# An adaLN transformer block on one core: in seven of sixteen blocks, exponentials straight from query-by-key scores, turned on VectorE and gathered through DRAM

## The chip, the cores and the metric

The kernel runs on one core of a Trainium2 chip. A core has five engines that run side by side, each in its own order: TensorE (PE in the profile; its weight loads stand as PEld), VectorE (DVE), ScalarE (ACT), GpSimd (POOL) and SyncE (SP), which here issues nearly all transfers. Sixteen DMA engines move the data. An engine waits for another by semaphores. The metric is the time of one execution in microseconds (us); lower is better. Before the change the median of three runs is 3510.68 us (3505.79 to 3512.32).

## What is computed

A transformer block with adaptive layer norm, in float32: batch 8, sequences of 1024 rows, width 512, 16 heads of 32, hidden width 2048. The attention is causal.

```
mod = silu(condition) @ Wada + bada
sh_a, sc_a, gt_a, sh_m, sc_m, gt_m = split(mod, 6)
xm = layernorm(x, g1, be1) * (1 + sc_a) + sh_a
q, k, v = heads(xm @ Wqkv)
scores = where(causal, q @ k.T * hd ** -0.5, -inf)
x = x + gt_a * (softmax(scores) @ v @ Wproj + bproj)
xm = layernorm(x, g2, be2) * (1 + sc_m) + sh_m
x = x + gt_m * (gelu(xm @ W1 + b1) @ W2 + b2)
```

## The kernel before

The rows are cut into 16 blocks `n` of 512, two to each batch: the even block is a sequence's first half, the odd one its second. The queries of an even block see the keys of their own block (a triangle of ten 128x128 tiles per head), those of an odd block see 26 tiles. The 16 heads stand in four groups `g` of four heads; a group's four heads take the 128 partitions, 32 each.

*Linear work.* The projections and the MLP go by Strassen products over halves (`strassen`, `down`), each matmul group through the helper at line 217 into one of three PSUM banks. Weights come in pieces of 256 KB through a ring of eight (`fetch`, line 347, the tile `w`): a piece's load is issued when the piece eight places before it has been used. Pre-added pieces of weights lie in DRAM (`kept_...`). Normalized rows are turned for the products by 32x32 blocks on VectorE (line 700, tile `hat` to `xm`), stored to DRAM (`held`) and loaded back in another order.

*Attention before.* The scores are computed twice. First by query and key (`scores_at_once`, tile `sc`, matmuls at line 1595): VectorE adds the causal mask on the diagonal (line 1607) and takes the maximum of each row (line 1610). The maxima are split into three bf16 parts (`split_maxima`), transposed by matmuls into rows (`maxima_rows`, line 1648) and copied to `mrow`. Then the scores by key and query (`weights_T`, tile `st`): a bf16 matmul puts the negated maxima in (line 1674), an f32 one adds the scores (line 1686), one ScalarE activation takes the exponentials of up to 4 x 512 columns (line 1698) into a page `pT`, and GpSimd sets what lies behind the diagonal to zero (line 1703). `weigh` multiplies page and values into `po` (line 1726). GpSimd adds the pages up (line 1816), `finish` sums the result over keys by matmuls with ones (line 1747), copies sums and outputs out of PSUM, inverts the sums on VectorE in four pieces (line 1765) and multiplies on GpSimd (line 1790). The result takes the place of the queries, and `project_out` reads it.

`sc` and `st` share one buffer of four PSUM banks (`ps_st`, one buffer), `po` is one bank, and there are three pages (`free_p`) of 8 KB per partition. A unit of work is one part of 512 columns or two parts that add up to 512 (the triangle's rows of 384 and 128, or the 256s of two neighbouring groups): five units for two groups of an even block.

*What sets the order.* The order of every engine's instructions is written out by a planner in the kernel: estimated costs (`note`, `note_act`, `note_dma`) give each buffer a due time, and at each step the planner takes attention or linear work, whichever waits least, keeping to a rate between the two (`step_aside`, line 1457; `pace`, line 1899). On the chip each engine then works off its own list in order. All transfers stand in SP's list, so a transfer that has to wait holds back those behind it, weights among them.

```
    ps_st = ctx.enter_context(tc.tile_pool(name="ps_st", bufs=1, space=PSUM))
    RING = 8
    free_p = list(range(3))
    TRIANGLE = [[0], [1, 3], [2]]
```

Of the kernel before, what the change touches and what calls it, by code (L numbers as in the profile page):

```python
# [22 lines left out]
def kernel(  # L23
# [414 lines left out]
    cond_act = tmp.tile([P, TB], F32, tag="top", name="cond_act", bufs=1)[:B, :]  # L438
# [118 lines left out]

    def run_jobs(everything=False):
# [37 lines left out]
    def hurry():  # L596

        while jobs and due(jobs[0][1]) <= now["PE"] + 500:
# [882 lines left out]
    groups = [(n, g) for n in range(NB) for g in range(NC)]  # L1481
# [177 lines left out]
    free_p = list(range(3))  # L1659
    first_end, unadded = (0, NC - 1), []  # L1660
    outs, totals = {}, {}

    def weights_T(n, g, parts):
# [31 lines left out]
        slot = free_p.pop(0)  # L1695
# [40 lines left out]
    def finish(n, g):  # L1736
# [15 lines left out]
        free_p.extend([slot, *(held for *_, held in more)])  # L1752
        top = tmp.tile([P, TB], F32, tag="top", name=f"top_{n}_{g}", bufs=1)
        rec = tmp.tile([P, TB], F32, tag="rec", name=f"rec_{n}_{g}", bufs=1)
# [28 lines left out]

        def quotient():
            invert(3)
# [33 lines left out]
    def attend():  # L1819
        previous = None  # L1820
        for n in range(NB):
            h = blocks[n][1]
            slots = []
            mine = sum(exp_need(parts) for g in range(NC) for parts in weight_units(n, g))
            for g in range(NC):
                nxt = groups.index((n, g)) + 1
                n_slots = len(weight_units(n, g))

                over = n_slots - 1 if g % 2 == 0 else n_slots
                for k in range(n_slots):  # L1830
                    upto = len(units)
                    if nxt < len(groups):
# [4 lines left out]
                        if k == n_slots - 1 and nxt + 1 < len(groups):  # L1837
# [3 lines left out]
            stream["rate"] = planned_time(n) / mine * (0.7 if n == 0 else 1.0)  # L1841
# [32 lines left out]
    def close(n, g, parts, pT, slot, last):  # L1874

        until(lambda: n - blocks[n][1] + parts[-1][0] // NTT in valued)
        own, other = [[part for part in parts if (part[3] == g) == of] for of in (True, False)]
# [3 lines left out]
        elif parts[0][0] > 0 and (n, g) != first_end:  # L1881
            free_p.append(slot)
        if parts[0][0] == 0:
            totals[n, g] = (pT, slot)
            if (n, g) in shared:
# [3 lines left out]
                if (n, g) != first_end:  # L1889
                    free_p.append(slot)  # L1890
        if last:
            finish(n, g)

# [17 lines left out]
    needs = sum(exp_need(parts) for n in range(NB) for g in range(NC) for parts in weight_units(n, g))  # L1911
    needs += sum(score_need(*unit) for unit in units)
# [81 lines left out]
```

## Time and profile before

| | |
|---|---|
| median of three runs | 3510.68 us (3505.79 to 3512.32) |
| profiled execution | 3510.74 us |
| its span | 3509.0 us |
| mean granted TensorE clock | 0.998 |
| matmuls of scores by query and key, line 1595 | 329.5 us busy |
| matmuls of scores by key and query, line 1686 | 300.8 us busy |
| exponentials, line 1698 | 540.9 us busy on ScalarE |
| additions of pages, line 1816 | 1219.7 us busy on GpSimd |
| moved by the DMA engines | 491.10 MB, 140 GB/s over the span |

A group of the profile names the line, the engine, the operation, what is written and read, the shapes and the number of records; then the busy time, the mean time of one in ns, and the idle time of the engine just before it with what ended it. An f32 matmul stands as two records. A line of the timeline has start, duration, engine, line, operation and count, and in brackets the idle time before it. A line of the windows has the window, its length, busy time and records of PE, PEld, VectorE, ScalarE and GpSimd, and at its end the granted clock, the DMA engines' busy share and GB/s.

### The profile page before, as it was taken

To read this page: it belongs to the slowest core of one execution; us is meant where nothing else is said; L and a number is where in the kernel's file an instruction comes from. 1 tells how busy PE (TensorE), PEld (TensorE's weight loads), DVE (VectorE), ACT (ScalarE), POOL (GpSimd) and SP (SyncE) were. 2 spreads that over 40 slices of the span, in tenths; PEclk is the share of its full clock that TensorE was granted. 3 is DMA by queue.
4 is the path that set the end of the run, shared out by engine and by line. 5 is a ranking of instruction groups with operands and counts; after the bars stand their busy time and mean duration, and the time that the engine had idled before them with its cause. 6 is when DMAs were issued, how large, how long until landed. Compare 5 with 4: busy or idle time off the path is not lost.

```text
span 3509.0 us, 120365 instructions
## 1 busy us (share of the span) xinstructions
PE 3454.3 (98%) x54429; PEld 1724.0 (49%) x54429; DVE 2198.9 (63%) x2401; ACT 1212.4 (35%) x1276; POOL 2084.2 (59%) x2258
## 2 busy tenths in 40 slices
PE   8999999999999999999999999999999999999999
PEld 4444445445554545445454454544555444554445
DVE  5766676564666656665666566765666756656563
ACT  2335333342233423335223342333423343232531
POOL 3767846666366663756727576275753658537660
PEclk9999999999999999999999999999999999999999
DMA  6843444535545445363454534545354544443334
GB/s 212 263 137 104 137 115 140 142 107 159 142 125 156 119 147 153 119 170 115 137 157 130 155 117 144 150 137 148 116 155 137 165 122 146 128 136 101 96 121 140
DMA packets 328194, 491.10 MB, mean 140 GB/s; under 512 B 27260, under 2 KB 177596, under 8 KB 324100
## 3 DMA queue, kind: packets, MB, share of 16 engines
q1 hardware_dynamic: 327568, 483.39, 47.1%
q8 instruction: 428, 7.01, 0.8%
q14 instruction: 82, 0.67, 0.1%
q10 hardware_dynamic: 116, 0.03, 0.0%
HBM read 425.57 MB, written 55.64 MB: 137 GB/s over the span
## 4 chain that ended last, share of the span: by engine, by line
PE 83%; POOL 7%; DMA 3%; DVE 3%; ACT 1%; issue 1%; SPq 1%; ACTq 0%; DVEq 0%; POOLq 0%
PE bank L217 59%; PE sc L1595 8%; PE st L1686 6%; PE po L1726 6%; POOL pT L1816 4%; PE st L1674 2%; PE bank L1747 2%; DMA hat_m<-held_m 1%; DVE mx L1610 1%; POOL hT L170 1%; ACT pT L1698 1%; DMA held_m<-xm_m 1%; PE bank L1648 0%; POOL xr L170 0%; DMA w<-in_L_cond_Wqkv_dram 0%
## 5 line engine op out<-in xcount | busy, mean ns | idle before, releaser
L1816 POOL TENSOR_TENSOR pT<-pT,pT 128x256 f32<-128x256 f32 (+3 forms) x1254 | 1219.7, 1007 | 298.5 <-PE po L1726 181.6
L1698 ACT ACTIVATE pT<-st 128x2048 f32<-128x2048 f32 x288 | 540.9, 1878 | 1065.1 <-PE st L1686 959.8
L217 PE MATMUL bank<-w,hT 128*32 128x256 f32 x14336 | 823.7, 380 | 0.4 <-issue 0.4
L1610 DVE TENSOR_REDUCE mx<-sc 128x4 f32<-128x2048 f32 (+3 forms) x384 | 665.9, 1755 | 235.6 <-PE sc L1595 229.5
L217 PEld LDWEIGHTS bank<-w,hT 128*32 128x32 f32 x14336 | 446.7, 110 | 390.3 <-issue 105.8
L217 PE MATMUL bank<-xm_m,w 128*32 128x256 f32 x8192 | 498.6, 381 | 3.6 <-ACT xm_m L774 2.2
L217 PE MATMUL bank<-t_m,w 128*32 128x256 f32 x6144 | 382.4, 380 | 0.9 <-DVE t_m L786 0.6
L217 PEld LDWEIGHTS bank<-xm_m,w 128*32 128x32 f32 x8192 | 255.6, 110 | 231.2 <-issue 62.2
L1703 POOL TENSOR_SCALAR_AFFINE_SELECT pT<-pT 128x512 f32<-128x512 f32 x256 | 167.5, 672 | 331.9 <-ACT pT L1698 329.4
L1607 DVE TENSOR_TENSOR sc<-sc,mask 128x1024 f32<-128x1024 f32 (+1 forms) x160 | 162.8, 1018 | 293.3 <-PE sc L1595 237.8
L1595 PE MATMUL sc<-kT,qT 32*128 32x512 f32 (+3 forms) x3072 | 329.5, 521 | 4.3 <-ACT pT L1698 3.3
L1726 PE MATMUL po<-pT,v 128*32 128x512 f32 (+3 forms) x3048 | 301.6, 490 | 3.9 <-POOL pT L1703 3.9
L1686 PE MATMUL st<-qT,kT 32*128 32x512 f32 (+3 forms) x3072 | 300.8, 487 | 0.0
L217 PEld LDWEIGHTS bank<-t_m,w 128*32 128x32 f32 x6144 | 189.6, 110 | 172.9 <-issue 48.5
L1765 DVE RECIPROCAL rec<-rec 128x128 f32<-128x128 f32 x256 | 227.3, 922 | 48.2 <-ACT rec L1756 48.2
L217 PE MATMUL bank<-xm_a,w 128*32 128x256 f32 x3968 | 243.4, 382 | 0.4 <-DMA w<-in_L_cond_Wqkv_dram 0.4
L217 PE MATMUL bank<-w,qT 128*32 128x512 f32 x2048 | 237.0, 595 | 1.1 <-DMA w<-in_L_cond_Wproj_dram 0.7
L1595 PEld LDWEIGHTS sc<-kT,qT 32*128 32x128 f32 x3072 | 129.6, 183 | 188.2 <-issue 88.4
L208 DVE TENSOR_TENSOR hT<-bank,u_u 128x512 f32<-128x512 f32 x187 | 126.6, 686 | 105.8 <-PE bank L217 103.1
L217 PE MATMUL bank<-t_a,w 128*32 128x256 f32 x2944 | 183.2, 380 | 0.0
L217 PEld LDWEIGHTS bank<-xm_a,w 128*32 128x32 f32 x3968 | 123.5, 110 | 110.3 <-issue 29.3
L1115 ACT ACTIVATE hT<-hT,cols 128x512 f32<-128x512 f32 x256 | 164.7, 712 | 35.9 <-DVE hT L208 28.5
(243 smaller groups left out, 3404.0 us busy)
## 6 DMA issues: line engine op xcount, KB each, us to landing
w<-in_L_cond_W_dram SPq DMA_DIRECT2D x384, 256.0 KB
w<-kept_up_S SPq DMA_DIRECT2D x256, 256.0 KB
w<-kept_down_S SPq DMA_DIRECT2D x256, 256.0 KB
w<-kept_qkv_S SPq DMA_DIRECT2D x180, 256.0 KB
w<-in_L_cond_Wqkv_dram SPq DMA_DIRECT2D x147, 256.0 KB
hat_a<-in_x_dram SPq DMA_DIRECT2D x64, 256.0 KB
xr<-in_x_dram SPq DMA_DIRECT2D x32, 512.0 KB
w<-in_L_cond_Wproj_dram SPq DMA_DIRECT2D x64, 256.0 KB
```

The lines of the kernel that those rows point to most:

```text
L208: nc.vector.tensor_tensor(out, src, other, op)
L217: nc.tensor.matmul(ps[r, :], columns, rhs, start=start, stop=stop, skip_group_check=True)
L1115: nc.scalar.activation(hT[:, i, :], hT[:, i, :], AF.Gelu, bias=cols[:, O_B1 + f : O_B1 + f + 1])
L1595: nc.tensor.matmul(sc[:, j, c0 : c0 + w], qTs[n][r, gg, ts(qt, P)], keys_of(n, kh)[r, gg, :w], start=True, stop=True, skip_group_check=True,)
L1607: nc.vector.tensor_tensor(place, place, shape_of.to_broadcast(place.shape), ALU.add)
L1610: nc.vector.tensor_reduce(maxima[n, gg][:, kh, qt, :], sc[:, :, c0 : c0 + w], axis=AX.X, op=ALU.max)
L1686: nc.tensor.matmul(st[:, j, c0 : c0 + w], kT[r, gg, ts(k % NTT, P)], qT[r, gg, TB - w :], start=False, stop=True, skip_group_check=True,)
L1698: nc.scalar.activation(pT[:, :, :used], st[:, :, :used], AF.Exp, scale=scale)
L1703: nc.gpsimd.affine_select(diagonal, diagonal, pattern=[[0, HPG], [1, P]], compare_op=ALU.is_ge, fill=0.0, base=0, channel_multiplier=-1,)
L1726: nc.tensor.matmul(po[r, TB - w :], v[:, k % NTT, g * P + j * hd : g * P + (j + 1) * hd], pT[:, j, c0 : c0 + w], start=(k == 0), stop=last ...
L1765: nc.vector.reciprocal(some, some)
L1816: nc.gpsimd.tensor_tensor(into, into, pT[:, j, c0 : c0 + w], ALU.add)
```

## The change

Blocks 2, 4, 6, 8, 10, 12 and 14 (`by_rows`) take another way. Their scores are computed once, by query and key, with mask and maxima on VectorE as before. ScalarE takes the exponentials from there at once, one activation per head and part, with the row's negated maximum as bias, the running sum as a second output, and the columns written in an order that suits the turning. VectorE turns the page by 32x32 blocks in place, four transfers per part scatter it to an image in DRAM, and three pages per group are gathered from there with the keys on partitions. Their matmuls with the values follow (six visits per head and group where there were four). The sums stay with the rows: they are inverted as 128x16, turned, and go through DRAM into a tile of the output's layout, which multiplies the output once.

For these blocks the second scores, the maxima's rows, the zeroing and adding of pages on GpSimd, the column sums and the four inversions per group fall away. The odd block behind such a block takes its first page to the values only when the block's last group is finished. Of its pace, 0.6 of the block's linear work goes beside the row units and the rest beside the next block. `top` and `rec` become two halves of one tile, and small jobs of VectorE may run up to 2 us ahead of PE.

```diff
+    def by_rows(n):
+        return n > 1 and blocks[n][1] == 0
+
-    groups = [(n, g) for n in range(NB) for g in range(NC)]
+    groups = [(n, g) for n in range(NB) for g in range(NC) if not by_rows(n)]
...
     def run_jobs(everything=False):
+        run_row_jobs(everything)
         while jobs and (
-            everything or (now["DVE"] <= now["PE"] and due(jobs[0][1]) <= now["PE"])
+            everything or (now["DVE"] <= now["PE"] + 2000 and due(jobs[0][1]) <= max(now["PE"], now["DVE"]))
...
+            if by_rows(n):
+                attend_rows(n, previous)
+                previous = None
+                continue
...
     def close(n, g, parts, pT, slot, last):
         until(lambda: n - blocks[n][1] + parts[-1][0] // NTT in valued)
+        if blocks[n][1] and by_rows(n - 1):
+            until(lambda: (n - 1, NC - 1) in gathered)
...
+    def rows_unit(n, g, parts):
+        until(lambda: n in projected)
+        until(lambda: free_p and len(raws) < 2)
+        slot = take_slot()
+        raws.append(slot)
...
+        for qt, kh, c0, w, gg in parts:
+            for j in range(HPG):
+                r = slice(j * hd, (j + 1) * hd)
+                nc.tensor.matmul(
+                    sc[:, j, c0 : c0 + w], qTs[n][r, gg, ts(qt, P)], kTs[n][r, gg, :w],
+                    start=True, stop=True, skip_group_check=True,
+                )
...
+        nc.vector.tensor_tensor(place, place, shape_of.to_broadcast(place.shape), ALU.add)
...
+            nc.vector.tensor_reduce(mx[:, i, :], sc[:, :, c0 : c0 + w], axis=AX.X, op=ALU.max)
...
+        nc.vector.tensor_scalar(minus[:, :n_parts], mx[:, :n_parts], -scale, None, ALU.mult)
...
+            for j in range(HPG):
+                nc.scalar.activation(
+                    tile_of[:, j], sc[:, j, c0 : c0 + w].rearrange("p (k b x) -> p k b x", b=NTT, x=hd),
+                    AF.Exp, bias=minus[:, i, j : j + 1], scale=scale, accum_out=totals_of[n, gg][:, j, qt : qt + 1],
+                )
...
+        def turned():
+            nc.vector.transpose(raw, raw)
+            start(scatter())
...
+                for a in range(NTT):
+                    into = images[n, gg][qt // 2][:, qt % 2, a, :count, :]
+                    nc.sync.dma_start(
+                        into.rearrange("(b k) s e -> k b (s e)", k=hd),
+                        raw[ts(a, hd), at : at + HPG * w].rearrange("k (b f) -> k b f", b=NTT),
+                    )
...
+    def inverses(n, g):
...
+        nc.vector.reciprocal(some, some)
+        wide = some.rearrange("p j t -> p (j t)").unsqueeze(2).to_broadcast([P, HPG * NTT, hd])
+        nc.vector.transpose(both[:, 1, :].rearrange("p (y i) -> p y i", i=hd), wide)
...
+        nc.sync.dma_start(
+            rows.rearrange("j t a i -> a (j t) i"),
+            both[0:P:hd, 1, :].rearrange("a (y i) -> a y i", i=hd),
+        )
...
+            nc.sync.dma_start(both[ts(j, hd), 0, :], row.to_broadcast([hd, TB]))
...
+    def gather(n, g):
...
+        moves = (
+            [((both,), high[:, :, :, :2, :].rearrange("p t a s e -> p (t a) s e"), 2900)],
+            [
+                ((second,), high[:, 1, :, 2:, :], 1450),
+                ((first, 0), high[:, 0, :, 2, :], 730),
+                ((first, 1), low[:, 1, :, 1, :], 730),
+            ],
+            [((both, 0), low[:, :, :, 0, :].rearrange("p t a e -> p (t a) e"), 1450)],
+        )
...
+                yield [("image", n, g), SLOT, PAGE, *before], []
+                if free_p and not (pages and n not in issued):
+                    break
...
+            for at, source, ns in moves[i]:
+                nc.sync.dma_start(page[(slice(None), *at)], source)
...
+                    nc.tensor.matmul(
+                        state["out"][r, qt * P : qt * P + wide],
+                        vs[n][:, k, g * P + j * hd : g * P + (j + 1) * hd],
+                        page[:, rows_of, at, r],
...
+    def finish_rows(n, g, out):
+        key, into, by = ("att", n), qTs[n][:, g, :], inverse_rows.pop((n, g))
+        ready = due(["top", "po"])
+        if max(now["DVE"], ready) > max(now["ACT"], ready) + 2500:
+            nc.scalar.copy(into, out)
+            either(into, into, by, ALU.mult, ["top"], [key])
+        else:
+            nc.vector.tensor_tensor(into, out, by, ALU.mult)
```

More of the change, by code (lines that the diff above doesn't have):

```diff
@@ L1659, with count_slots, take_slot, give_slot @@
     free_p = list(range(3))
+    SLOT, PAGE = "a page", "a page to turned rows"
+    all_issued, pages = [True], []
+    def count_slots():
+        written[SLOT] = 0.0 if free_p else NEVER
+        written[PAGE] = NEVER if pages and not all_issued[0] else 0.0
+    def take_slot():
+        slot = free_p.pop(0)
+        count_slots()
+        return slot
+    def give_slot(slot):
+        free_p.append(slot)
+        count_slots()
     first_end, unadded = (0, NC - 1), []
@@ L1751, in finish @@
             note_pe(2 * COLUMN * w, "columns", [("acc", n, g), ("p", held)], [("l", bank)])
[L1752 to L1754 removed]
+        for one in (slot, *(held for *_, held in more)):
+            give_slot(one)
+        both = tmp.tile([P, 2, TB], F32, tag="top", name=f"top_rec_{n}_{g}", bufs=1)
+        top, rec = both[:, 0, :], both[:, 1, :]
         kr = "rec"
@@ L1782, in finish @@
             return
+        written["top used"] = NEVER
         def quotient():
+            written["top used"] = 0.0
             invert(3)
@@ new lines, in finish_rows @@
+    def finish_rows(n, g, out):
[3 more added lines that the diff above has]
+            nc.scalar.copy(into, out)
+            note_act(585, None, ["po"], [key])
+            either(into, into, by, ALU.mult, ["top"], [key])
+        else:
+            nc.vector.tensor_tensor(into, out, by, ALU.mult)
+            note("DVE", 690, ["po", "top"], [key])
+        written["spread", n, g] = 0.0
+        gathered.add((n, g))
+        if g == NC - 1:
+            written["attended", n] = 0.0
```

187 lines of the change are left out of this document (178 added, 9 removed).

## The prediction

> **What bounds the kernel now.** I read the engines' shares first, then PE's waits, then PE's groups by shape.
>
> ```profile
> span 3509.0 us, 120365 instructions
> PE 3454.3 (98%) x54429; PEld 1724.0 (49%) x54429; DVE 2198.9 (63%) x2401; ACT 1212.4 (35%) x1276; POOL 2084.2 (59%) x2258
> ```
>
> TensorE is busy for 3454.3 of 3509.0 us, and no other engine passes 63%. So a PE instruction that goes away takes its time off the end, and any wait given to PE instead is paid in full. The change is therefore a trade: matmuls taken from PE in seven blocks, against new waits of PE on a long way through the other engines and DRAM. The profiled execution took 3510.74 us (1.7 us around the span), the median of the runs is 3510.68: the sum below starts at 3510.7.
>
> **The change part by part. Matmuls that go.** The groups of PE by shape (busy us and mean ns of one):
>
> ```profile
> L1726 PE MATMUL po<-pT,v 128*32 128x512 f32 x1528 | 200.9, 597 | 3.2 <-POOL pT L1703 3.2
> L1686 PE MATMUL st<-qT,kT 32*128 32x512 f32 x1536 | 198.0, 590 | 0.0
> L1674 PE MATMUL st<-mrow,minus_ones 32*128 32x512 bf16 x768 | 76.0, 386 | 7.5 <-DVE mx L1610 6.9 <-ACT mrow L1654 0.4
> L1747 PE MATMUL bank<-pT,ones 128*32 128x512 f32 x512 | 75.0, 593 | 1.0 <-POOL pT L1816 0.9
> L1686 PE MATMUL st<-qT,kT 32*128 32x384 f32 x512 | 55.6, 509 | 0.0
> L1726 PE MATMUL po<-pT,v 128*32 128x384 f32 x504 | 52.8, 491 | 0.5 <-POOL pT L1703 0.5
> L1726 PE MATMUL po<-pT,v 128*32 128x256 f32 x512 | 39.7, 382 | 0.0
> L1686 PE MATMUL st<-qT,kT 32*128 32x256 f32 x512 | 33.1, 375 | 0.0
> L1648 PE MATMUL bank<-ident_b,mcols 128*32 128x128 bf16 x1024 | 26.2, 220 | 3.9 <-POOL mcols L1632 3.3 <-DVE hT L208 0.4
> L1726 PE MATMUL po<-pT,v 128*32 128x128 f32 x504 | 25.3, 273 | 0.2 <-POOL pT L1703 0.2
> L1686 PE MATMUL st<-qT,kT 32*128 32x128 f32 x512 | 24.9, 269 | 0.0
> L1674 PE MATMUL st<-mrow,minus_ones 32*128 32x384 bf16 x256 | 21.9, 332 | 1.0 <-DVE mx L1610 0.9
> L1674 PE MATMUL st<-mrow,minus_ones 32*128 32x128 bf16 x256 | 14.3, 214 | 0.0
> L1674 PE MATMUL st<-mrow,minus_ones 32*128 32x256 bf16 x256 | 12.7, 273 | 0.0
> ```
>
> Seven blocks of four groups lose, per group, four matmuls of each of the four widths; an f32 matmul stands as two records, so 224 records of each width go, and 112 of the bf16 ones. Busy per record is busy over count. Scores by keys (L1686): 224 x (0.129+0.109+0.065+0.049) = 78.6 us. Maxima into them (L1674): 112 x (0.099+0.086+0.050+0.056) = 32.5. Column sums (L1747): 224 x 0.146 = 32.8. Maxima turned to rows (L1648): 448 x 0.0256 = 11.5. The scores by queries stay, under another name. The weighted values are the same columns cut otherwise (896 records of 256 and 448 of 128 for 224 of each width): 69.4 + 22.5 against 81.5, +10.4. Together 145.0 us, as busy time. That is too much, since a group's tail overlaps the next group's head:
>
> ```profile
> 703.65 0.40 PE L1674 MATMUL st<-mrow,minus_ones 32*128 32x512 bf16 x4
> 703.87 1.03 PE L1686 MATMUL st<-qT,kT 32*128 32x512 f32 x8
> 704.83 0.64 PE L1726 MATMUL po<-pT,v 128*32 128x512 f32 x4
> ```
>
> Here a weight unit holds PE from 703.65 to 704.83, 1.18 us, where its busy times add up to 1.43: a factor 0.825, which makes 145 into 120. I take 120, and keep 145 as the upper end.
>
> **The way of a row unit.** Rows for its steps:
>
> ```profile
> L1610 DVE TENSOR_REDUCE mx<-sc 128x4 f32<-128x2048 f32 x192 | 439.8, 2291 | 232.3 <-PE sc L1595 229.5
> L1607 DVE TENSOR_TENSOR sc<-sc,mask 128x1024 f32<-128x1024 f32 x96 | 118.2, 1232 | 170.1 <-PE sc L1595 126.6 <-issue 21.6 <-ACT top L1759 13.4
> L1115 ACT ACTIVATE hT<-hT,cols 128x512 f32<-128x512 f32 x256 | 164.7, 712 | 35.9 <-DVE hT L208 28.5 <-POOL hT L170 6.7
> L677 ACT ACTIVATE rstd_m<-mv_m,eps 128x1 f32<-128x1 f32 x4 | 1.2, 295 | 17.9 <-DVE mv_m L675 12.2 <-DVE rstd_m L682 3.6 <-DVE offset_m L683 2.0
> ```
>
> The exponentials by query need a bias per head, so four or eight small ones replace one of 2048 columns. No row shows an exponential with a running sum; its bounds are 0.30 us (one column) and 0.71 (512 columns with a bias), in between by width, and I take 0.71, 0.61, 0.50, 0.40 for 512, 384, 256, 128. One unit then holds the only score buffer for its matmuls (1.1), mask (0.7 or 1.2), maxima (2.3 or 2.4) and exponentials (2.9 or 4.0): 7 us for one part, 9 for two, ten units 82 us a block. PE fills that with projections and MLP wherever the built order has some between.
>
> Behind it stand VectorE's turning of 2048 columns, the scatter to DRAM and the gathers. The nearest row is how the normalized rows go the same way, 1 MB out and back:
>
> ```profile
> 827.81 2.43 DVE L700 STREAM_TRANSPOSE xm_a<-hat_a 128x512 f32<-128x512 f32 x4
> 830.48 0.42 SPq L709 DMA_DIRECT2D held_a<-xm_a  x1
> 835.61 2.79 SPq L714 DMA_DIRECT2D hat_a<-held_a  x4
> 845.36 2.93 ACT L774 ACTIVATE xm_a<-hat_a,shifta,gaina 128x512 f32<-128x512 f32 x4 [2.62 <-DMA hat_a<-held_a]
> ```
>
> Turning four times 512 columns takes 2.43 us, and from the store's issue to data back 14.9. So from the end of a group's last score matmuls to its first page: 3.7 + 4.0 + 2.4 + 14.9 = 25 us (20 if SP is free, 35 if other transfers stand ahead).
>
> I weigh that against the built order of the changed kernel, taking each PE instruction start to start. In blocks 4 to 14 the work between a group's last score matmuls and its first page is 31 to 56 us: covered. In block 2 it is 13 us, because the output projection of block 1 stands there, itself behind block 1's last quotient; from the block's first row unit to the first page PE has 25 us of work where three units (9+7+9), turning and the round trip need 42. So PE stands 17 us there, and about 4 more at pages that come 3 us behind one another, since a second page is asked for only when the first has been used.
>
> **A standing PE costs more than its wait.** Granted clock is the third column from the end:
>
> ```profile
> 215.00:220.00 5.00, 2.33 (x16) 1.09 (x20) 3.90 (x3) 0.20 (x1) 4.68 (x8) 0.76 0.19 53
> 220.00:225.00 5.00, 5.00 (x26) 1.01 (x18) 3.05 (x3) 2.58 (x2) 5.00 (x4) 0.56 0.02 5
> 218.81 0.62 PE L1674 MATMUL st<-mrow,minus_ones 32*128 32x512 bf16 x4 [2.41 <-DVE mx L1610]
> 219.19 1.94 PE L1686 MATMUL st<-qT,kT 32*128 32x512 f32 x8
> ```
>
> PE stood 2.41 us, and then the same eight matmuls took 1.94 us in place of 1.03. The missing clock is 5 x (0.24 + 0.44) = 3.4 us. The Trainium skill, "TensorE: Matmul & The Clock Gate" (Part 1: The HAM clock gate), states that an idle window of about 3.4 us halves the clock until a busy one has passed; the trace agrees in size, though the gap here was 2.41 us. By the page alone a wait of 3 us would leave the clock as it is, and the late pages among the rivals would come to 3440 - 21 + 72 = 3491. I add 3.4 us for each wait of that length, two in block 2: 17 + 4 + 7 = 28 us (bounds 10 and 45). In the six other blocks the shortest distances between pages are 5 us (blocks 4 and 6) and a leg of the round trip is about 7, so I give them 3.5 us each, 21 in all (bounds 0 and 90).
>
> **What lies beside other work.** VectorE loses 112 reciprocals and gains 70 turnings:
>
> ```profile
> L1765 DVE RECIPROCAL rec<-rec 128x128 f32<-128x128 f32 x256 | 227.3, 922 | 48.2 <-ACT rec L1756 48.2
> q1 hardware_dynamic: 327568, 483.39, 47.1%
> 844.00:850.00 6.00, 5.97 (x104) 3.20 (x100) 2.94 (x5) 3.40 (x5) 0.91 (x1) 1.00 1.06 368
> 840.00:844.00 4.00, 4.00 (x80) 2.39 (x76) 0.79 (x2) 0.59 (x1) 2.56 (x2) 1.00 1.07 208
> ```
>
> 112 x 0.922 = 103 us less and 70 x 2.43 = 170 more; with some fifty copies that the built order moves over from ScalarE at 0.69, VectorE comes to some 2300 us, under 70%. GpSimd only loses. Both hide under PE. The DMA engines are nearer their limit. A group's weights are 2.62 MB, written once and read once: 28 x 5.24 = 147 MB on 483. At the present 0.471 x 3509 / 483.39 = 3.42 us per MB that is 18 us a group, 72 a block, within the 186 us of PE work from a block's first row unit to its last page; with the 47% that are there already, 86% of the engines. Stretches of full load do not stop PE by themselves: in the two windows above all DMA engines are busy and PE too. SP issues 728 more DMAs; at 0.42 that is 306 us over seven blocks on a queue that carries the weights' loads, which are asked for eight pieces ahead, some 15 us of PE work. That cover is what hides them; a scatter that waits for its turning longer than that stops PE for the difference.
>
> **The sum.** 3510.7 - 120 + 28 + 21 = 3440 us.
>
> **The rivals.** *All hidden.* The rows allow it: cover exceeds 25 us in six blocks, and PE waits for DMA almost nowhere now. Then only matmuls count: 3510.7 - 120 = 3390, or with 145 and block 2's lower bound 3376. Against it stands the order of block 2. *The DMA engines bind.* This ends on the other side. The window from 840 is a load into 32 partitions at a time at 208 GB/s, the one behind it runs at 368; the scatters read 32 partitions at a time. At 208 GB/s both ways a group takes 25 us, a block 101, and 87 are already asked for in 186: exactly full. From there each us a group costs 28 us in all, and from 27.5 us the saving is gone; at 30, with weights queued behind, 3440 + 140 = 3580. Against it: the gathers fill all 128 partitions. *Each group's first page comes late*, by 3 us in all six blocks, with the clock lost behind it: 24 x 6.4 = 154, 3440 - 21 + 154 = 3573, slower too. It decides where the round trip takes 10 us more than the row. *Less goes than is said*: exponentials with sums at twice my price (1.2 us a unit's head) make units 11 to 13 us, 30 us a block more on the score buffer, of which PE can fill most; at 8 us a block, 3440 + 56 = 3496.
>
> **How the numbers follow.** Forecast 3440 with its own range 3400 to 3480: 0.52. All hidden: 0.20. DMA binds: 0.14. Late first pages: 0.05. Dear exponentials: 0.09. Below 3503.7 (0.2%, about what a measurement of this kernel can tell) lie the first two and half of the last: faster 0.77; same 0.04; slower 0.19. Range 3376 to 3520: it takes in the hidden case and stops between the dear and the DMA case, leaving out a little under 2 in 10.
>
> **What would show it.** PE's busy time near 3310 to 3340 us; scores by keys down from 3072 records to 2176; waits of PE for the gathered pages ("turned") over 2 us in block 2 and rare later, with the granted clock under 1 only there. Waits of PE for weights ("w") and a DMA share near 1 through the row stages would show the DMA case; waits for VectorE's maxima or ScalarE's exponentials spread over all blocks, the dear ones. The forecast is wrong if PE's idle time passes 150 us, or if busy time stays above 3370.

## The result, and the profile after

The changed kernel takes 3544.72 us (median of four runs, 3542.93 to 3549.06) against 3509.31 for the kernel before: a ratio of 1.0104, 95% interval 1.0089 to 1.0119. It is slower by 35 us; the forecast was 3440, the range ended at 3520. The profiled execution took 3545.22 us, its span is 3543.5. From its page (span, busy time of the engines, and the DMA queue that carries the data):

```profile
span 3543.5 us, 118795 instructions
PE 3377.7 (95%) x52861; PEld 1705.4 (48%) x52861; DVE 2339.5 (66%) x2562; ACT 1248.8 (35%) x1970; POOL 1762.9 (50%) x1710
...
q1 hardware_dynamic: 501952, 637.80, 60.8%
```

PE's busy time fell by 76.6 us (3454.3 to 3377.7) and its idle time rose from 54.7 to 165.8 us, by 111.1: together the 34.5 us by which the span grew. The busy time hides a second loss. The mean granted clock is 0.985 after 0.998, and where the trace's stretches of half clock overlap with busy matmuls, half of that overlap is lost: added up, 37 us now, 5 before. So matmuls worth some 108 us went, 32 came back as slow clock, 111 as standing. Who PE waited for (total us, times, longest):

```profile
PE bank L217 <- DMA w<-in_L_cond_W_dram: 19.7, 3, 7.5
PE po L2155 <- DMA turned<-image: 17.1, 19, 3.2
PE bank L217 <- DVE xm_a L782: 16.3, 2, 8.6
PE bank L217 <- DMA w<-in_L_cond_Wproj_dram: 16.2, 11, 4.5
PE rows_sc L2021 <- ACT rows_p L2040: 12.5, 4, 7.9
PE st L1709 <- DVE mx L1628: 8.9, 11, 2.6
```

Before, no single wait was over 3.1 us but the one for the condition (6.5). Now the waits for two kinds of weights (`W`, `Wproj`) make 36 us, those for the normalized rows that return from DRAM (`xm_a`) 16, the gathered pages only 17: most of the new waits hit linear work that the change didn't touch. They lie where the row blocks run. Four stretches of 100 us (busy time of PE, PEld, VectorE, ScalarE, GpSimd; at the end clock, DMA share, GB/s), first before, then after:

```profile
400.00:500.00 100.00, 99.57 (x1492) 47.28 (x1492) 67.75 (x77) 34.12 (x35) 64.54 (x94) 1.00 0.38 114
1700.00:1800.00 100.00, 99.60 (x1576) 50.00 (x1568) 62.01 (x75) 24.88 (x28) 50.45 (x69) 1.00 0.48 138
3000.00:3100.00 100.00, 100.00 (x1584) 50.17 (x1580) 57.37 (x70) 32.74 (x37) 42.84 (x64) 1.00 0.43 127
```

```profile
400.00:500.00 100.00, 78.41 (x1039) 36.09 (x1032) 65.23 (x75) 34.00 (x101) 33.78 (x35) 0.88 0.66 198
900.00:1000.00 100.00, 94.22 (x1600) 53.77 (x1596) 64.28 (x86) 30.87 (x68) 8.03 (x10) 0.98 0.83 240
1700.00:1800.00 100.00, 94.00 (x1528) 50.38 (x1524) 72.32 (x89) 24.68 (x80) 35.47 (x26) 0.97 0.91 274
3000.00:3100.00 100.00, 87.84 (x1416) 47.25 (x1412) 64.02 (x82) 23.47 (x72) 31.74 (x26) 0.98 0.95 281
```

The work in a stretch isn't the same in both kernels; what can be read is the level. In the last three the DMA engines are 83 to 95% busy, and PE stands for 6 to 12 us in 100; over all stretches of 100 us behind 500 with a share over 0.8 it is 4 to 16. The first one (400 to 500) is a case of its own, with 0.66 and 21.6 us.

Inside the stretch from 3000 the chain of what ended last (start, us, what) goes through one round trip of normalized rows, then through weights:

```profile
3072.41 10.48 DMA held_m<-xm_m
...
3084.95 7.19 DMA hat_m<-held_m
...
3092.20 6.07 DMA w<-in_L_cond_W_dram
```

The store takes 10.48 us, the last reading back 7.19, and the first weights of the MLP, issued only at 3092.20, another 6.07. PE had run out of work at 3090.93 and stood through one of the longest of the waits above:

```profile
3098.40 1.94 PE L217 MATMUL bank<-xm_m,w 128*32 128x256 f32 x16 [7.48 <-DMA w<-in_L_cond_W_dram]
```

These weights were issued late: in SP's list they stand behind three gathers and the four reads of the inverted sums, all new with the change.

```profile
3082.97 2.41 SPq L728 DMA_DIRECT2D hat_m<-held_m  x4
3085.43 1.53 SPq L2143 DMA_DIRECT2D turned<-image  x3
3087.78 3.46 SPq L2105 DMA_DIRECT2D inverse<-inverse_rows  x4
3092.20 1.88 SPq L358 DMA_DIRECT2D w<-in_L_cond_W_dram  x2
```

In this program SP's transfers signal eight semaphores in turn, and each waits until the one eight places ahead of it has landed. So the weights waited for the last reading of `hat_m`, which they don't read; it landed at 3092.14, and they were issued 0.06 us later. All three waits of the `W` line, 19.7 us, have this form: the same seven transfers stand ahead, and the load was issued 0.1 to 1.3 us after PE had run out of work. The rows that PE needed too had landed no earlier than 3092.14, so an earlier load would have saved at most some 5 of the 7.5 us here.

The round trip of the rows can be timed in each kernel from the store's issue to ScalarE's first use of the rows. Before:

```profile
3038.50 0.42 SPq L709 DMA_DIRECT2D held_m<-xm_m  x1
3051.93 2.23 ACT L774 ACTIVATE xm_m<-hat_m,shiftm,gainm 128x512 f32<-128x512 f32 x3 [1.94 <-DMA hat_m<-held_m]
```

After:

```profile
3072.41 1.02 SPq L723 DMA_DIRECT2D held_m<-xm_m  x1
3092.25 2.22 ACT L788 ACTIVATE xm_m<-hat_m,shiftm,gainm 128x512 f32<-128x512 f32 x3 [4.13 <-DMA hat_m<-held_m]
```

It is 13.4 us before and 19.8 after. Over the twelve such trips that fall into the row stages of blocks 4 to 14, the median is 20.5 us, and 14.8 for the same twelve before. During such a trip the engines are nearly full in the kernel before too (first row before, second after):

```profile
3038.00:3052.00 14.00, 14.00 (x256) 7.64 (x252) 9.72 (x12) 1.83 (x4) 8.81 (x12) 1.00 0.88 258
3072.00:3092.00 20.00, 17.31 (x320) 11.32 (x309) 4.15 (x6) 1.76 (x3) 0.00 (x0) 1.00 0.96 271
```

At 258 and 271 GB/s that makes 3.6 and 5.4 MB: the longer trip has more bytes moved while it is under way. The single packets are no slower; those of 2 KB take 114 ns on average before and 111 after.

The new operations cost what they were priced at or less (exponentials, turning; the scores by keys with their count):

```profile
L2040 ACT ACTIVATE rows_p<-rows_sc,rows_minus 128x256 f32<-128x256 f32 (+3 forms) x448 | 229.6, 534 | 448.0 <-DVE rows_minus L2034 246.4
L1721 PE MATMUL st<-qT,kT 32*128 32x512 f32 (+3 forms) x2176 | 228.5, 508 | 0.0
...
L2053 DVE STREAM_TRANSPOSE rows_p<-rows_p 128x2048 f32<-128x2048 f32 x70 | 160.9, 2298 | 36.2 <-ACT rows_p L2040 35.5
```

### The profile page after: what moved, and what is told of

The parts are those of the page before. It is cut to its first block, busy times and chain, and to the rows that moved or that the text cites. A ratio compares the mean times of both kernels' runs of the same rounds, so it can differ in the third digit from the quotient of the medians.

```text
span 3543.5 us, 118795 instructions
## 1 busy us (share of the span) xinstructions
PE 3377.7 (95%) x52861; PEld 1705.4 (48%) x52861; DVE 2339.5 (66%) x2562; ACT 1248.8 (35%) x1970; POOL 1762.9 (50%) x1710
## 4 chain that ended last, share of the span: by engine, by line
PE 37%; DMA 6%; POOL 4%; DVE 3%; issue 1%; SPq 1%; ACT 1%; DVEq 0%; POOLq 0%; ACTq 0%
PE bank L217 27%; PE sc L1613 3%; POOL pT L1856 3%; PE po L1762 2%; PE st L1721 2%; DMA held_m<-xm_m 1%; DMA turned<-image 1%; PE rows_sc L2021 1%; PE st L1709 1%; PE po L2155 1%; DVE mx L1628 1%; DMA w<-in_L_cond_Wproj_dram 1%; DMA hat_m<-held_m 1%; PE bank L1783 0%; DMA w<-in_L_cond_W_dram 0%
## 5 line engine op out<-in xcount | busy, mean ns | idle before, releaser
L1856 POOL TENSOR_TENSOR pT<-pT,pT 128x512 f32<-128x512 f32 (+3 forms) x918 | 981.9, 1104 | 250.5 <-ACT pT L1734 197.2
L1734 ACT ACTIVATE pT<-st 128x2048 f32<-128x2048 f32 x218 | 409.5, 1879 | 762.1 <-PE st L1721 573.9
L217 PEld LDWEIGHTS bank<-w,hT 128*32 128x32 f32 x14336 | 457.0, 110 | 372.7 <-issue 87.5
L1628 DVE TENSOR_REDUCE mx<-sc 128x4 f32<-128x2048 f32 (+3 forms) x271 | 499.4, 1859 | 183.0 <-PE sc L1613 179.7
L217 PE MATMUL bank<-xm_m,w 128*32 128x256 f32 x8192 | 506.6, 384 | 28.8 <-DMA w<-in_L_cond_W_dram 19.7
L2040 ACT ACTIVATE rows_p<-rows_sc,rows_minus 128x256 f32<-128x256 f32 (+3 forms) x448 | 229.6, 534 | 448.0 <-DVE rows_minus L2034 246.4
L217 PE MATMUL bank<-xm_a,w 128*32 128x256 f32 x3968 | 252.1, 392 | 26.0 <-DVE xm_a L782 16.3
L217 PE MATMUL bank<-w,qT 128*32 128x512 f32 x2048 | 242.0, 610 | 16.3 <-DMA w<-in_L_cond_Wproj_dram 16.2
L1613 PE MATMUL sc<-kT,qT 32*128 32x512 f32 (+3 forms) x2168 | 250.6, 546 | 6.9 <-DVE mx L1628 3.5
L1762 PE MATMUL po<-pT,v 128*32 128x512 f32 (+3 forms) x2176 | 232.0, 515 | 4.5 <-POOL pT L1739 4.4
L1721 PE MATMUL st<-qT,kT 32*128 32x512 f32 (+3 forms) x2176 | 228.5, 508 | 0.0
L2053 DVE STREAM_TRANSPOSE rows_p<-rows_p 128x2048 f32<-128x2048 f32 x70 | 160.9, 2298 | 36.2 <-ACT rows_p L2040 35.5
L1625 DVE TENSOR_TENSOR sc<-sc,mask 128x1024 f32<-128x1024 f32 (+1 forms) x89 | 90.5, 1017 | 124.4 <-PE sc L1613 91.9
L1129 ACT ACTIVATE hT<-hT,cols 128x512 f32<-128x512 f32 x256 | 164.4, 711 | 22.8 <-DVE hT L208 21.6
```

Of the source, the lines that this page charges most:

```text
L217: nc.tensor.matmul(ps[r, :], columns, rhs, start=start, stop=stop, skip_group_check=True)
L1129: nc.scalar.activation(hT[:, i, :], hT[:, i, :], AF.Gelu, bias=cols[:, O_B1 + f : O_B1 + f + 1])
L1613: nc.tensor.matmul(sc[:, j, c0 : c0 + w], qTs[n][r, gg, ts(qt, P)], keys_of(n, kh)[r, gg, :w], start=True, stop=True, skip_group_check=True,)
L1625: nc.vector.tensor_tensor(place, place, shape_of.to_broadcast(place.shape), ALU.add)
L1628: nc.vector.tensor_reduce(maxima[n, gg][:, kh, qt, :], sc[:, :, c0 : c0 + w], axis=AX.X, op=ALU.max)
L1721: nc.tensor.matmul(st[:, j, c0 : c0 + w], kT[r, gg, ts(k % NTT, P)], qT[r, gg, TB - w :], start=False, stop=True, skip_group_check=True,)
```

## The experiments

Theory A: the load of the scatters and gathers on the DMA engines makes the other transfers late, weights and normalized rows above all, and PE stands although no single engine is full. Theory B: not the bytes but SP's one list holds the weights back, behind transfers that wait for VectorE's turning. Beside these stood three smaller suspects: the new rule for VectorE's small jobs, the entry into the first row block (theory C below; for the quarter of the bytes, C is the order and latency of the whole chain), and the planner's idea of how long a transfer takes.

| run | us (median) | ratio to before, 95% interval |
|---|---|---|
| changed kernel | 3544.7 | 1.0104 [1.0089, 1.0119] |
| half of the new bytes | 3498.0 | 0.9969 [0.9960, 0.9979] |
| a quarter of the new bytes | 3483.8 | 0.9930 [0.9911, 0.9950] |
| kernel before with copies beside it | 3563.4 | 1.0160 [1.0145, 1.0175] |
| new transfers issued by GpSimd | 3651.8 | 1.0406 [1.0388, 1.0423] |
| without row blocks, other edits kept | 3532.5 | 1.0069 [1.0054, 1.0084] |
| row blocks with the old rule for small jobs | 3571.5 | 1.0188 [1.0170, 1.0205] |
| the same with half of the bytes | 3529.1 | 1.0070 [1.0053, 1.0087] |
| block 2 by the old way | 3561.2 | 1.0145 [1.0130, 1.0161] |
| all linear work beside the row units | 3562.6 | 1.0159 [1.0144, 1.0174] |
| planner's transfers x0.8 | 3647.7 | 1.0385 [1.0368, 1.0402] |
| planner's transfers x1.3 | 3600.2 | 1.0264 [1.0248, 1.0279] |
| planner's transfers x1.6 | 3811.5 | 1.0862 [1.0843, 1.0881] |

**Half of the bytes, then a quarter.** The order of all instructions stays; scatter, gather and product take 64, then 32 of the 128 partitions.

```diff
-                        into.rearrange("(b k) s e -> k b (s e)", k=hd),
-                        raw[ts(a, hd), at : at + HPG * w].rearrange("k (b f) -> k b f", b=NTT),
+                        into.rearrange("(b k) s e -> k b (s e)", k=hd)[:, :2],
+                        raw[ts(a, hd), at : at + HPG * w].rearrange("k (b f) -> k b f", b=NTT)[:, :2],
...
-                nc.sync.dma_start(page[(slice(None), *at)], source)
+                nc.sync.dma_start(page[(slice(0, P // 2), *at)], source[: P // 2])
...
-                        vs[n][:, k, g * P + j * hd : g * P + (j + 1) * hd],
-                        page[:, rows_of, at, r],
+                        vs[n][: P // 2, k, g * P + j * hd : g * P + (j + 1) * hd],
+                        page[: P // 2, rows_of, at, r],
```

The quarter has `:1` and `hd` (32) in these places.

> The changed kernel with half of each scatter and each gather: 64 of 128 partitions of the images are written and read, and the matmuls of gathered pages read 64 partitions. Same instructions on every engine, same order, same semaphores; about 73 MB fewer moved, and half of the keys are missing from the row blocks' outputs. Theory A, the load of the DMA engines makes weights, normalized rows and pages late: PE idle falls from 166 us to 100 or less, the granted clock rises from 0.985 to 0.993 or more, time 3430 to 3475 us. Theory B, transfers that wait in SP's list hold the weights back whatever their size: idle stays over 140 us, time 3520 to 3545 us. Theory C, the order of block 2 is the loss: as B, with only the waits of other blocks a little shorter, 3510 to 3540 us.

> The changed kernel with a quarter of the new transfers' partitions: 32 of 128 are scattered, gathered and multiplied; the order of the instructions is as it was, and only a quarter of the keys enters the outputs of the row blocks. Half of the bytes gave 3498 us against 3545, 47 us less. Theory A (the load on the DMA engines delays the weights, the normalised rows and the pages): another quarter of the bytes away gives about half as much again, 3465 to 3485 us, with PE idle for 85 to 105 us. Theory C (what is left is the order and the latency of the chain from exponentials to pages, which bytes do not change): 3490 to 3505, with PE idle still near 115 us.

Half of the bytes takes 47 us off, the quarter 61. The half, at 3498.0, lies outside every range on record, above A's and below those of B and C, and PE's idle time (116 us) is above A's 100; the quarter, at 3483.8, lies inside A's range, with 106 us of idle time against 105 at most. The same four stretches with a quarter:

```profile
400.00:500.00 100.00, 79.20 (x989) 34.41 (x984) 68.08 (x75) 34.13 (x102) 32.87 (x35) 0.85 0.40 116
900.00:1000.00 100.00, 98.78 (x1707) 53.49 (x1701) 69.92 (x91) 36.24 (x75) 13.04 (x15) 1.00 0.66 188
1700.00:1800.00 100.00, 97.43 (x1540) 48.97 (x1536) 66.31 (x87) 21.80 (x64) 24.97 (x22) 0.97 0.70 201
3000.00:3100.00 100.00, 99.16 (x1676) 52.82 (x1668) 68.38 (x85) 31.46 (x72) 12.35 (x13) 1.00 0.65 186
```

The last three are back at 97 to 99% with the DMA engines at 65 to 70% (of those not shown, 800 to 900 and 1300 to 1400 stay at 93 and 94%). The first one has not gained: its loss doesn't hang on the bytes. The round trip of the rows is down to 16.2 us (17.7 in the median of the twelve):

```profile
3023.76 0.42 SPq L723 DMA_DIRECT2D held_m<-xm_m  x1
3039.96 2.23 ACT L788 ACTIVATE xm_m<-hat_m,shiftm,gainm 128x512 f32<-128x512 f32 x3 [0.23 <-DMA hat_m<-held_m]
```

And in PE's groups by shape (idle time before them behind the last bar) the waits for weights are all but gone, 2.7 and 2.8 us where the changed kernel has 19.7 and 16.2:

```profile
L217 PE MATMUL bank<-xm_m,w 128*32 128x256 f32 x8192 | 503.1, 382 | 7.5 <-DMA w<-in_L_cond_W_dram 2.7 <-ACT p_u L197 1.4 <-DVE p_u L194 1.4
L217 PE MATMUL bank<-w,qT 128*32 128x512 f32 x2048 | 238.0, 603 | 2.9 <-DMA w<-in_L_cond_Wproj_dram 2.8
```

This also speaks against theory B as it was put. SP's list is the same, and SP waited for the turned pages even longer with a quarter (first row) than in the changed kernel (second):

```profile
SPq L2068 <- DVE rows_p L2053: 37.5, 14, 7.6
```

```profile
SPq L2068 <- DVE rows_p L2053: 29.9, 13, 7.1
```

So it isn't SP's waiting for VectorE that costs PE the time. This doesn't clear SP's list as a whole. The same seven transfers stand ahead of the late weights, and with a quarter those three waits make 2.7 us instead of 19.7. From 400 us on, SP's issues of weights were held for the landing of other transfers for 5 us in the kernel before, 63 in the changed one, 56 with half and 14 with a quarter. So the bytes act partly through the list: with more of them landings come later, and the list passes that on. No run changes one and not the other.

The share of the DMA queue times the span gives 1817, 1984 and 2154 us per engine for quarter, half and whole. The upper 170 us cost 47 us, the lower 167 only 14, with 6 to 8 us of uncertainty on each by the intervals. By bytes the two steps are less far apart, since the first is 73 MB and the second 37: 0.64 and 0.39 us per MB.

**The load alone, on the kernel before.** In the even blocks from 2 on each unit of weights issues two copies of 1 MB from DRAM to DRAM, 140 in all; nothing waits for them.

```diff
+        if n > 1 and not h:
+            for i in range(2):
+                copied = kept.tile([1024, 256], F32, tag=f"copied_{n}_{g}_{parts[0][0]}_{i}", name=f"copied_{n}_{g}_{parts[0][0]}_{i}")
+                nc.sync.dma_start(copied, x[blocks[n][0], i * TB : (i + 1) * TB, :].rearrange("t (a d) -> (t a) d", a=2))
```

> The kernel before with 140 copies of 1 MB from DRAM to DRAM in runs of 1 KB, two beside each weight unit of blocks 2, 4 to 14, nothing waiting for them: 147 MB more through the DMA engines, as many as the change moves, and the order of every engine's other work as before. Theory A, the load alone makes PE stand: 3550 to 3610 us, with PE's waits for weights and normalized rows going up. Rival, what makes PE stand is the chain of the row units (the way out and back and what queues for it), not the load: 3510 to 3525 us.

It costs 57 us, inside A's range, on a kernel whose other engines do nothing new. From its page and PE's waits:

```profile
PE 3470.1 (97%) x54429; PEld 1736.5 (49%) x54429; DVE 2198.0 (62%) x2401; ACT 1212.9 (34%) x1276; POOL 2084.9 (59%) x2258
...
q1 hardware_dynamic: 332048, 630.20, 57.0%
```

```profile
PE bank L217 <- ACT xm_m L774: 13.4, 3, 7.5
...
PE bank L217 <- DMA w<-in_L_cond_W_dram: 7.0, 1, 7.0
```

The same victims, normalized rows and weights, with single waits of 7 us. Added load suffices for a loss of the size that the bytes have in the changed kernel; no scatter waiting for VectorE is needed. But it isn't the same load: 147 MB against the change's 154, 378 us per engine against 502, and in packets of 64 KB (2240 of them, 2.8 us each; the expectation has runs of 1 KB) where the change's have 0.5 to 2 KB. The copies stand in SP's list too, and weights were held for landings for 49 us. So the run shows that load can cost this much, not that the change's 154 MB do so in the same way.

**The new transfers on GpSimd's list** (four issues moved):

```diff
-                    nc.sync.dma_start(
+                    nc.gpsimd.dma_start(
...
-            nc.sync.dma_start(both[ts(j, hd), 0, :], row.to_broadcast([hd, TB]))
+            nc.gpsimd.dma_start(both[ts(j, hd), 0, :], row.to_broadcast([hd, TB]))
...
-                nc.sync.dma_start(page[(slice(None), *at)], source)
+                nc.gpsimd.dma_start(page[(slice(None), *at)], source)
```

> The changed kernel with all new transfers (scatters, gathers, the sums' two legs) issued from GpSimd's queue instead of SP's; bytes, shapes and the order on the other engines as in the changed kernel. Theory B: weights are no longer held back in SP's list, PE's waits for w fall from 44 us to under 15 us, time 3470 to 3510 us. Theory A: the DMA engines have the same load, PE's waits for weights and pages stay at 60 us or more, time 3530 us or more, later still where GpSimd is slower at issuing them.

107 us more, and PE's waits for pages go from 17.1 to 84.4:

```profile
PE po L2155 <- DMA turned<-image: 84.4, 29, 9.4
...
PE bank L217 <- DMA w<-in_L_cond_Wproj_dram: 13.7, 4, 8.7
...
PE bank L217 <- DMA w<-kept_qkv_S: 9.0, 4, 4.3
```

This doesn't decide on B by itself, since GpSimd comes to its issues late. With SP's list free of the new transfers PE's waits for weights are 29 us in all, against 44. The waits for `W`, 19.7 us in the changed kernel, are gone, as they should be if the seven transfers ahead of them were their cause; at the same three places PE stood 2 to 6 us for something else. The other weights came late all the same. The Trainium skill, "DMA: Bandwidth & Descriptors" (Issuing engines are not separate DMA queues), says that transfers of any issuing engine run on the same 16 engines and mix there; the trace agrees in so far as the two queues together take 44.0 + 14.4 = 58.4% of 3651.0 us, 2132 us per engine, where the one took 2154.

**The rule for VectorE's small jobs**, kept without row blocks, and taken back with them:

```diff
-        return n > 1 and blocks[n][1] == 0
+        return False
```

```diff
-            everything or (now["DVE"] <= now["PE"] + 2000 and due(jobs[0][1]) <= max(now["PE"], now["DVE"]))
+            everything or (now["DVE"] <= now["PE"] and due(jobs[0][1]) <= now["PE"])
```

> No block goes by rows; the other edits of the change stay (small VectorE jobs up to 2 us ahead of PE, one tile for top and rec, the waits for a page written out). Theory 'the loss is in the row stages': 3505 to 3520 us, PE idle about 55 us, as before the change. Rival 'the edits that all blocks share cost': 3525 to 3545 us, PE idle over 75 us, and the new waits would be found in stages without row units too.

> The changed kernel with the rule of before for VectorE's small jobs (none while VectorE's list is ahead of PE's). With no block by rows this rule alone cost 23 us (3532.5 against 3509.7), and undoing it there gives back the order of before. Theory 'the rule's loss adds to that of the rows': 3515 to 3530 us. Rival, the rule is needed by the row stages, whose turnings queue behind other jobs: 3540 us or more.

Without row blocks the rule costs 23 us: it reorders a plan that needed no look-ahead. PE's idle time there is 64 us, 9 more than before and below the 75 of the expectation; another 9 are lost to a slower clock. With row blocks the rule is worth 27. Under the old one PE's waits for pages (33.2 us) and for the rows `xm_a` (24.6) are longer than under the new (17.1 and 16.3). So the rule isn't what makes the change slow. Half of the bytes with the old rule (both edits above) showed that the load's price doesn't hang on this order:

> Half of the bytes and VectorE's old rule together: as the run with half of each scatter and gather (half of the keys missing from the row blocks' outputs), with the small jobs of VectorE placed as before the change. If the load of the DMA engines (47 us for half of it) and the rule (23 us) are separate losses they add: 3470 to 3482 us. If the rule's loss is a part of what the load does, or the row stages need the rule: 3490 to 3505 us.

It gives 42 us (3571.5 to 3529.1), where the new rule's order gave 47. The time itself lies above both ranges on record, since with row blocks the old rule costs 27 us instead of saving 23.

**The entry into the row blocks.** Block 2 goes by the old way, the first row block is block 4:

```diff
-        return n > 1 and blocks[n][1] == 0
+        return n > 2 and blocks[n][1] == 0
```

> Six blocks by rows instead of seven; block 2 goes the old way. Its idle time of 25 us (400 to 600 us of the profile) and the clock lost behind it (12 us) go, and its saving of about 17 us with them. Theory C: 3515 to 3530 us, idle near 140 us. Theories A and B: the same 20 us at most, and the idle time of 10 to 16 us in each of the blocks 4 to 14 stays as it was, so the time stays above 3510 us.

16.4 us slower than with block 2, about what a block's matmuls are worth (108 / 7 = 15.4). Theory C's 3515 to 3530 is out. Block 2 pays for its own wait, and leaving it out frees nothing: the wait moves to block 4, where one piece of 12.0 us makes nearly all of this line:

```profile
PE rows_sc L2021 <- ACT rows_p L2040: 12.6, 3, 12.0
```

**All of a block's linear work beside its row units** (`SHARE = 0.6` to `1.0`) was to give the round trips more cover:

> The changed kernel with SHARE 1.0 in place of 0.6: a row block's units are spread over all of its linear work, so the same bytes move over a longer stretch. Theory A, the load of the DMA engines while the row units run: the share of the DMA engines in the row stages falls from 0.85 to 0.95 to under 0.8, PE waits less for weights and normalized rows, 3500 to 3530 us. Rival, what is put off comes back: the odd block's attention gets less linear work beside it, PE waits there for maxima and exponentials, time at or above 3545 us.

18 us slower. The DMA engines' share didn't fall as A wanted: it is 0.82 to 0.92 in the stretches of 100 us where it was 0.81 to 0.95. The rival's waits for maxima and exponentials grow by some 9 us, of the 21 by which PE's idle time grows. So this way of spreading the work doesn't help; whether cover is short it doesn't show.

**The planner's idea of a transfer.** The edit for 1.3; 1.6 and 0.8 stand in the same place.

```diff
-        now["DMA"] = max(begun + BEGIN, now["DMA"]) + ns
+        now["DMA"] = max(begun + BEGIN, now["DMA"]) + 1.3 * ns
```

> The changed kernel, complete; only the planner is told that every DMA takes 1.3 times as long, about what the packets of 2 KB take in the changed kernel (111 ns on average against a median of 84). If the planner's wrong idea of the load places pages, weights and dependent products too early, telling it gives fewer waits for pages and weights and 3505 to 3530 us. If the order cannot get round the load (the transfers are late because the engines are full, wherever the products stand): 3535 to 3560.

> As the run with 1.3, with DMA durations of 1.6 in the planner. If a wrong idea of the load is the cause, this is as good as 1.3 or better, 3500 to 3530; if the order cannot get round the load, 3535 to 3570.

> The changed kernel, complete; the planner is told that every DMA takes 0.8 times as long. With 1.3 times it took 55 us more and with 1.6 times 267 more, so a higher price is no remedy. If the planner's price was already too high (it puts work off for transfers that have landed), 0.8 gives 3515 to 3535 us, below the 3545 of the changed kernel. If the price of the changed kernel is near the best for its order and the rest is load, which the order cannot get round: 3540 to 3580, with more waits for pages and weights than the 17 and 36 us of the changed kernel.

The price as it was is the best of the four: 103 us more at 0.8, 55 at 1.3, 267 at 1.6. No expectation had effects of that size. At 0.8 PE's waits for pages and for weights of the output projection grow to

```profile
PE po L2155 <- DMA turned<-image: 104.3, 47, 11.5
PE bank L217 <- DMA w<-in_L_cond_Wproj_dram: 34.5, 10, 11.9
```

At 1.6 the waits for pages are 129.9 us; at 1.3 they stay at 19.1, and many smaller waits grow. The load wasn't planned away by any of these factors. Whether an order by hand could do better is open. No version here that computes the whole reference beats the kernel before.

## Why the prediction was wrong

*Matmuls that go: right in mechanism, 12 us too high.* 120 forecast, 108 measured; the scores by keys went from 3072 records to the 2176 forecast. That is 0.745 of the 145, so the factor 0.825, read from one unit, was too high.

*Block 2: 28 us, right in size, in part by luck, and wrong in place.* From 420 to 480:

```profile
420.00:450.00 30.00, 17.16 (x164) 6.34 (x160) 21.94 (x23) 11.27 (x42) 3.51 (x4) 0.72 0.64 188
450.00:480.00 30.00, 24.82 (x298) 10.52 (x292) 22.16 (x29) 10.78 (x41) 7.35 (x9) 0.90 0.83 252
```

PE stands 12.8 + 5.2 = 18 us, against 17 + 4 forecast, and 0.28 x 30 + 0.10 x 30 = 11.4 us of clock are missing, partly while it stood, against 7. But it doesn't stand at the first page; it stands at the one score buffer, which the exponentials hold:

```profile
425.51 1.71 PE L2021 MATMUL rows_sc<-kT,qT 32*128 32x512 f32 x8 [2.60 <-ACT rows_p L2040]
...
444.36 2.09 PE L2021 MATMUL rows_sc<-kT,qT 32*128 32x512 f32 x8 [7.87 <-ACT rows_p L2040]
...
461.45 1.07 PE L2155 MATMUL po<-turned,v 128*32 128x256 f32 x16 [0.65 <-DMA turned<-image]
```

From the block's first row unit (416.46) to its first page (461.45) it is 45 us, where 42 were counted, and PE is busy for 30.6 of them, some at half clock, where 25 were counted. So the chain and the work were nearly right, and with them the standing; but the wait came earlier, and for the page PE waited only 0.65 us. There is luck in the size: without row blocks, under the new rule for small jobs, PE stands 6.8 us in the stretch from 400 to 500 too, and that had no price in the sum.

*The step that failed: "Stretches of full load do not stop PE by themselves", and the 21 us built on it.* The DMA engines' load itself was well sized: 504 us forecast per engine (147 MB at 3.42 us), 502 measured (2154 less 1653), as 154 MB at 3.25; the sums' 8 MB were left out. What was wrong was to call it hidden at 86% because there was room, from two windows of 4 and 6 us in which PE evidently had what it needed. The 86% is a mean over a block. While a trip is under way the engines are near full already in the kernel before (0.88 in the trip at 3038), so what is added beside it makes it longer: 20.5 us for 14.8 in the median. The covers, read from the built order, were held against the trip of the kernel before, 14.9. With three quarters of the bytes gone 61 us of the loss go too, and about as many bytes put on the kernel before cost 57. The loss fell on weights and normalized rows as much as on the new pages, so 3.5 us for each of six blocks, counted at pages alone, had the wrong victims: outside 400 to 500 the idle time grew by some 90 us (111.1 less the 21.2 by which PE's busy time in that stretch fell). That is already the upper bound of this term, 90, and lost clock comes on top.

*"That cover is what hides them", of SP's new transfers and the ring of eight, failed with it.* Single waits for weights reach 7.5 us. The prediction allowed for scatters that wait for their turning, and the quarter speaks against those. Two other things stand in their place. Loads take longer: from 400 to 3300 us the slowest tenth of the weights' loads takes over 5.2 us from issue to landing before, over 7.1 after. And the three longest of those waits come from loads issued late, behind gathers and reads of the sums that were held for landings in their turn. Moving those weights ahead in the list wasn't tried, so how the 61 us divide between the two is open.

*A term left out.* The look-ahead for VectorE's small jobs had no price in the sum. It costs 23 us in the order without row blocks. How much of that remains in the changed kernel can't be read from two runs of opposite sign.

*Right:* exponentials (534 ns on average; priced at 0.40 to 0.71 us), turning (2.30 us for 2.43), VectorE (2339.5 us for some 2300), and that a standing PE loses clock behind its wait, though 7 us were priced and 32 more than before were lost. Among the rivals "The DMA engines bind" had the right cause with the wrong threshold: it wanted 25 us a group to be exceeded, and below that gave nothing; a group took 17.9 (502 / 28). Both signs named beforehand for a wrong forecast came: idle time over 150 us (165.8) and busy time over 3370 (3377.7).

*What is open.* With a quarter of the new bytes 24 us are gained where 108 us of matmuls went. The stretch of the entry holds 20 of the missing 84 us as standing (99.57 less 79.20) and part of 15 us of clock; the remaining quarter, the rule and the reordered stages share the rest, and no run parts these. Open too is which part of the bytes' 61 us goes through SP's list.

## What to carry over

Mean room on the DMA engines is no cover: read their share while the trips that matter are under way (here 0.88 where the mean was 0.47), and count on what is added beside them making them longer (here 14.8 us to 20.5). Look first at the transfers that the change doesn't touch, weights and round trips among them, and at what newly stands ahead of them in the issuing list. Where a change trades matmuls for bytes, put about those bytes as idle copies beside the old kernel first: one run gives a first price of the trade. An edit that only changes the order can cost as much as one that adds work, and needs a term of its own.

## What the runs showed of the hardware

Half of a transfer's partitions took more than half of its engine time: of the 502 us per engine that the change added, 331 were left with half of the scatters' and gathers' bytes and 164 with a quarter (the sums' 8 MB stayed whole). Issued by GpSimd, the gathers of 1024 KB took 7.9 us in the median from issue to landing (KB each, median us):

```profile
turned<-image POOLq DMA_DIRECT2D x28, 1024.0 KB, 7.9
```

Short waits also cost clock: at 425.51 above a wait of 2.60 us was followed by eight matmuls in 1.71 us; elsewhere in the same kernel they take 1.14:

```profile
887.27 1.14 PE L2021 MATMUL rows_sc<-kT,qT 32*128 32x512 f32 x8
```

The Trainium skill, "TensorE: Matmul & The Clock Gate" (Part 1: The HAM clock gate), gives an idle window of some 3.4 us as what halves the clock; here, as in the kernel before, less was enough. The stretches at half clock last 3.4, 6.8 or 10.2 us in these two traces, but for the last, which the kernel's end cuts off; the 3.4 us that the prediction sets beside the page's window are what a stretch of 6.8 us costs.
